# Scan layers of a hybrid network: every engine issues in the program's order instead of the scheduler's order

## Chip, cores, metric

The kernel runs on one core of a Trainium2 chip. The metric is the device time of the execution in microseconds (us). A program on one core has no second core to compare itself with, so the state of a run is read from its time and its granted TensorE clock; every run told here was a fast one and gave the reference's result.

Engines are named as in the profile: PE is TensorE's matmul, PEld its weight load, DVE is VectorE, ACT is ScalarE, POOL is GpSimd and SP is SyncE.

## The reference

Two layers with a selective scan over images of 64 x 64, then two attention and feed-forward layers on the same pixels as tokens. Only the scan layers are touched. Per image (four of them), per layer:

```python
xs = [x_hw, x_wh, x_hw reversed, x_wh reversed]          # k: four directions, L = 4096
dts, B, C = split(einsum("kdl,kcd->kcl", xs, x_proj))     # 6, 16, 16
delta = softplus(einsum("krl,kdr->kdl", dts, dt_w) + dt_b)
h = exp(delta * A) * h + delta * B * u                    # one step along L, 192 x 16 states
y = (h * C).sum(states)                                   # summed over the directions
```

and then a normalisation, a gate silu(z) and an output projection.

## The kernel before

An image is 32 **scan steps**: four directions k, each of eight chunks of 512 pixels. A step has six **groups** g0 to g5 (halves h of the channels, blocks i of the states). A group passes through all engines. The program writes the stages of different groups in a software pipeline: while group n is scanned, n-1 is weighed by C, n-2 is summed, n-3 is kept, and the next step's inputs are made in three small pieces per group. The scheduler may reorder the instructions of an engine where no data forbids it, and did so.

```python
p_da = ...bufs=4, space=PSUM     # exp(delta*A), one bank per tile of a group
p_y = ...bufs=1, space=PSUM      # y_ps
p_b = ...bufs=2, space=PSUM      # b_ps
p_one = ...bufs=1, space=PSUM    # "ps1": everything else on PE
...
def chunk_inputs(xc, k, c, got):           # a generator: each yield is one piece
    u = scan_view(xc, k, c)                # strided in the transposed directions
    got["b"] = p_b.tile(...); c_ps = p_one.tile(...)
    ... four matmuls with bc_w: b, then c
    yield
    got["c"] = cp.tile([128, TC], F32, name="cc", bufs=2)
    nc.scalar.copy(got["c"], c_ps)
    yield
    for m in range(2):
        raw = p_one.tile([128, TC], F32, name="ps1")
        ... two matmuls with dl_w (L229)
        yield
        nc.scalar.activation(top[:, m], raw, AF.Relu, ...)
        nc.scalar.activation(e[:, m], raw, AF.Abs, ...)
        yield
    ... ACT: exp, ln, identity             # yield
    nc.vector.scalar_tensor_tensor(w, ...) # L244; yield
    nc.gpsimd.tensor_tensor(...)           # x2, delta; yield; yield
    ... du = delta * u on DVE (L253), and its transfer to DRAM

class Group:
    def scan(self):
        for t in range(NT):                # NT = 4
            da = p_da.tile([128, TC], F32, name="da")
            nc.tensor.matmul(da, cst.rep[part, i], self.got["delta"][part, h], ...)
        for t, da in enumerate(das):
            nc.scalar.activation(da, da, AF.Exp, scale=a_col[...])
        for t in range(NT):
            nc.vector.tensor_tensor(st[:, t], st[:, t], self.got["b"], ALU.mult)
        for t, da in enumerate(das):
            nc.vector.tensor_tensor_scan(st[:, t], da, st[:, t], 0.0 if c == 0 else col, ...)
    def weigh(self):
        if c < NC - 1:
            nc.scalar.copy(self.carry[...], st[:, :, TC - 1])
        for t in range(NT):
            nc.gpsimd.tensor_tensor(st[:, t], st[:, t], self.got["c"], ALU.mult)
    def sum(self):
        if i == 0:
            y_of[h] = p_y.tile([P, TC], F32, name="y_ps")
        ... four matmuls into y_of[h]
    def keep(self):                        # only after the third block, i == 2
        nc.vector.tensor_tensor(to, to, rows(y_of[h]), ALU.add)
...
def stages(n):
    for back, stage in ((1, "weigh"), (3, "keep"), (2, "sum")):
        getattr(flat[n - back], stage)()
for n in range(len(steps)):
    ahead = chunk_inputs(xc, *steps[n + 1], inputs[n + 1])
    for at in range(n * 6, (n + 1) * 6):
        ... load the states of later groups
        flat[at].scan()
        stages(at)
        for _ in range(3):
            next(ahead, None)
```

Of the kernel before, what the change touches and what calls it, by code (L numbers as in the profile page):

```python
# [57 lines left out]
def rows(t):  # L58

    if len(t.shape) == 2:  # L60
        return t.rearrange("p (r w) -> p r w", w=HW)
    return t.rearrange("p h (r w) -> p h r w", w=HW)


class Consts:
# [29 lines left out]
def ssm_layer(ctx: ExitStack, tc, cst, a, pre, x_in, x_out):  # L95

    nc = tc.nc
# [45 lines left out]
    for k in range(K):  # L143
        for h in range(2):
# [7 lines left out]
            )  # L152
            nc.scalar.copy(dl_w[:, k, h], ps[:, : 2 * P])

    stats_of = {}

    def conv(b):
# [7 lines left out]
        for c in range(NC):  # L165
            mid = xn[:, 1 + ROWS * c : 1 + ROWS * (c + 1), 1 : 1 + HW]
            nc.sync.dma_start(mid, rows(x_in[b, :, c * TC : (c + 1) * TC]))
            nc.vector.bn_stats(st[:, c, :], mid)  # L168
# [20 lines left out]
        for c in range(NC):  # L189
            for h in range(2):  # L190
                ps = p_one.tile([128, TC], F32, name="ps1")
                for tap in range(9):
                    dy, dx = divmod(tap, 3)
                    nc.tensor.matmul(  # L194
                        rows(ps),
                        taps[:, tap, h * P : (h + 1) * P],
                        xn[:, ROWS * c + dy : ROWS * (c + 1) + dy, dx : dx + HW],
                        start=tap == 0,
                        stop=tap == 8,
                    )  # L200
                nc.scalar.activation(  # L201
                    xc[:, h, c * TC : (c + 1) * TC], ps, AF.Silu, bias=conv_b[:, h : h + 1]
                )
        return xc

    def chunk_inputs(xc, k, c, got):
# [5 lines left out]
        for m, ps in enumerate((got["b"], c_ps)):  # L212
            for h in range(2):
                nc.tensor.matmul(rows(ps), bc_w[:, k, h, m], u[:, h], start=h == 0, stop=h == 1)  # L214
# [45 lines left out]
    class Group:  # L260
# [6 lines left out]
        def __init__(self, k, c, h, i, got, carry, xc, y):  # L267
            self.k, self.c, self.h, self.i = k, c, h, i
            self.got, self.carry, self.xc, self.y = got, carry, xc, y
# [293 lines left out]
def body(tc, a, out):  # L563
    nc = tc.nc
    with ExitStack() as ctx:
        cst = Consts(nc, ctx.enter_context(tc.tile_pool(name="const", bufs=1)), a)
        dram = ctx.enter_context(tc.tile_pool(name="dram", bufs=1, space=DRAM))
        x1 = dram.tile([B, C, L], F32, name="x1")
        x2 = dram.tile([B, C, L], F32, name="x2")
        ssm_layer(tc, cst, a, "L0_", a["x"], x1)  # L570
        ssm_layer(tc, cst, a, "L1_", x1, x2)
        token_layers(tc, cst, a, ["L2_", "L3_"], x2, out)
# [85 lines left out]
```

## Time and profile before

| | before |
|---|---|
| time, median of 2 | 17766.17 us (17765.54 to 17766.8) |
| busy: PE, DVE, ACT, POOL | 14593.3, 13631.7, 7698.0, 8983.9 us |
| one scan step, median of the eight images | 51.84 us |
| from an image's last scan to the next one's first, median | 358.2 us |
| mean PE clock | 0.716 |

A "step" is the time from the first scan of an image to the end of its last, over 32. PE has the highest busy share, but DVE is what the scan waits for. The busy times in the four directions of the first image show it. The columns of this view are the stretch, its length in us, the busy us (and instructions) of PE, PEld, DVE, ACT and POOL, then the PE clock, the busy share of the DMA engines and GB/s. Before:

```profile
214.74:614.51 399.77, 353.74 (x866) 96.09 (x870) 382.49 (x421) 185.78 (x306) 274.08 (x206) 0.69 0.60 133
614.51:1042.61 428.10, 378.34 (x904) 94.37 (x900) 397.56 (x425) 192.07 (x315) 280.79 (x208) 0.72 0.57 126
1042.61:1454.00 411.39, 367.38 (x908) 100.56 (x900) 388.79 (x428) 192.49 (x314) 278.68 (x208) 0.68 0.59 131
1454.00:1873.20 419.20, 368.18 (x866) 89.61 (x862) 387.71 (x416) 200.58 (x318) 274.43 (x205) 0.72 0.55 121
```

Length less DVE's busy time, over eight steps, is DVE's stall per step: 2.2, 3.8, 2.8 and 3.9 us. Directions 2 and 4 read the image transposed.

### The profile page before, as it was taken

Reading aid. Unit: us, or ns where it says so; the run is one execution under the profiler, and the core shown is the slowest. Engines: PE = TensorE matmul, PEld = TensorE weight load, DVE = VectorE, ACT = ScalarE, POOL = GpSimd, SP = SyncE. Lnnn points to the kernel's source line nnn. Section 1 sums busy time; section 2 is a strip of 40 time slices with the busy share of each in tenths; the row PEclk is TensorE's granted clock in tenths of the full one; section 3 lists DMA queues with packets and bytes.
Section 4 is the critical chain, followed back from the end, with each engine's and each line's share of the span. In section 5 each row is a group of like instructions: output and inputs, shape, how many; then the busy total and the mean of one; then the engine's idle time right before and its main releaser. Section 6 shows DMA issues by size and latency. Waiting matters only on the chain.

```text
span 17763.9 us, 120237 instructions
## 1 busy us (share of the span) xinstructions
PE 14593.3 (82%) x34144; PEld 4171.9 (23%) x34144; DVE 13631.7 (77%) x15421; ACT 7698.0 (43%) x12017; POOL 8983.9 (51%) x6700
## 2 busy tenths in 40 slices
PE   8888788887888788887888788887888788885555
PEld 2222222222222222222222222222222222222222
DVE  5999399975999489984999579993999669993333
ACT  3444344443444344442444344442444334444555
POOL 3666166653666266652666356661666346660000
PEclk8767777667767777677776777677767777676665
DMA  4555165543555155542555255552555345550000
GB/s 88 129 128 128 40 133 129 128 98 74 129 128 129 41 126 129 128 106 62 133 124 131 60 109 127 130 122 48 131 128 129 71 96 128 129 126 23 7 7 7
DMA packets 360991, 1786.21 MB, mean 101 GB/s; under 512 B 93550, under 2 KB 94960, under 8 KB 162760
## 3 DMA queue, kind: packets, MB, share of 16 engines
q1 hardware_dynamic: 353160, 1765.94, 44.8%
q10 hardware_dynamic: 7168, 12.59, 0.2%
q8 instruction: 275, 4.51, 0.1%
q14 instruction: 388, 3.18, 0.1%
HBM read 1658.82 MB, written 119.54 MB: 100 GB/s over the span
## 4 chain that ended last, share of the span: by engine, by line
PE 41%; POOL 18%; DVE 17%; issue 15%; ACT 9%; DMA 0%; DVEq 0%; POOLq 0%; SPq 0%; ACTq 0%
POOL st L306 13%; PE da L285 11%; DVE st L297 9%; PE y_ps L313 8%; PE ps L194 6%; PE b_ps L214 5%; PE ps L229 4%; DVE st L293 3%; POOL delta L248 3%; POOL t L246 3%; ACT L88 1%; ACT da L291 1%; PE ps L362 1%; PE ps L370 1%; PE y_ps L383 1%
## 5 line engine op out<-in xcount | busy, mean ns | idle before, releaser
L306 POOL TENSOR_TENSOR st<-st,cc 128x512 f32<-128x512 f32 x6144 | 7785.6, 1298 | 4253.5 <-ACT carry L304 2489.1
L297 DVE TENSOR_TENSOR_SCAN st<-da,carry,st 128x512 f32<-128x512 f32 x5376 | 6460.2, 1264 | 662.8 <-ACT da L291 661.6
L285 PE MATMUL da<-delta,rep 32*128 32x512 f32 x12288 | 5498.9, 884 | 812.6 <-DVE st L297 723.7
L291 ACT ACTIVATE da<-da,A_logs 128x512 f32<-128x512 f32 x6144 | 3907.5, 664 | 4885.7 <-PE da L285 4876.1
L313 PE MATMUL y_ps<-st,sel 128*32 128x512 f32 x12288 | 3321.2, 913 | 798.5 <-POOL st L306 626.8
L293 DVE TENSOR_TENSOR st<-st,b_ps 128x512 f32<-128x512 f32 x6144 | 3788.2, 678 | 0.0
L285 PEld LDWEIGHTS da<-delta,rep 32*128 32x128 f32 x12288 | 1744.2, 245 | 4783.9 <-DVE st L297 3466.9
L229 PE MATMUL ps<-xc,dl_w 128*128 128x512 f32 x2048 | 1445.5, 834 | 23.5 <-ACT cc L217 12.6
L313 PEld LDWEIGHTS y_ps<-st,sel 128*32 128x32 f32 x12288 | 486.1, 137 | 3388.2 <-POOL st L306 1708.4
L246 POOL TENSOR_TENSOR t<-t,t 128x1024 f32<-128x1024 f32 x256 | 603.3, 2357 | 1047.5 <-DVE t L244 1047.5
L194 PE MATMUL ps<-xn,taps 96*128 96x512 f32 x2304 | 1047.4, 609 | 93.2 <-ACT xc L201 68.4
L214 PE MATMUL b_ps<-xc,bc_w 128*128 128x512 f32 x1024 | 980.8, 1052 | 73.5 <-DVE st L293 73.5
L253 DVE TENSOR_TENSOR du<-delta,xc 128x512 f32<-128x512 f32 x512 | 870.3, 1739 | 178.3 <-POOL delta L248 177.7
L237 ACT ACTIVATE t<-ps,dt_projs_bias 128x512 f32<-128x512 f32 x512 | 351.7, 687 | 1373.1 <-PE ps L229 1324.1
L297 DVE TENSOR_TENSOR_SCAN st<-da,st 128x512 f32<-128x512 f32 x768 | 876.2, 1201 | 50.5 <-ACT da L291 49.9
L214 PE MATMUL ps<-xc,bc_w 128*128 128x512 f32 x1024 | 874.4, 987 | 27.9 <-ACT t L238 21.7
L160 POOL MEMSET xn<- 96x66 f32 x8 | 1.2, 150 | 1762.7 <-PE ps L194 1598.0
L168 DVE BATCH_NORM_STATS2 st<-xn 96x6 f32<-96x512 f32 x64 | 44.2, 690 | 871.9 <-DMA xn<-x 437.2
L244 DVE SCALAR_TENSOR_TENSOR t<-t,t 128x1024 f32<-128x1024 f32 x256 | 329.3, 1286 | 426.0 <-ACT t L242 426.0
L484 POOL MEMSET tn<- 1x4096 f32 x8 | 28.0, 3506 | 1194.7 <-PE pa L525 1027.6
L229 PEld LDWEIGHTS ps<-xc,dl_w 128*128 128x128 f32 x2048 | 398.0, 205 | 949.8 <-issue 600.4
L248 POOL TENSOR_TENSOR delta<-t,t 128x1024 f32<-128x1024 f32 x256 | 600.7, 2347 | 3.1
(118 smaller groups left out, 8712.8 us busy)
## 6 DMA issues: line engine op xcount, KB each, us to landing
st<-scratch SPq DMA_DIRECT2D x1536, 1024.0 KB
scratch<-du SPq DMA_DIRECT2D x1024, 96.0 KB
xr<-in_x SPq DMA_DIRECT2D x64, 192.0 KB
x<-xr ACTq DMA_DIRECT2D x64, 192.0 KB
xr<-x SPq DMA_DIRECT2D x64, 192.0 KB
xn<-in_x SPq DMA_DIRECT2D x32, 192.0 KB
xn<-x SPq DMA_DIRECT2D x32, 192.0 KB
t<-x SPq DMA_DIRECT2D x4, 1536.0 KB
```

The costliest lines, as they stand in the source:

```text
L194: nc.tensor.matmul(rows(ps), taps[:, tap, h * P : (h + 1) * P], xn[:, ROWS * c + dy : ROWS * (c + 1) + dy, dx : dx + HW], start=tap == 0, ...
L214: nc.tensor.matmul(rows(ps), bc_w[:, k, h, m], u[:, h], start=h == 0, stop=h == 1)
L229: nc.tensor.matmul(rows(raw), dl_w[:, k, h, m * P : (m + 1) * P], u[:, h], start=h == 0, stop=h == 1,)
L246: nc.gpsimd.tensor_tensor(ln, ln, w, ALU.subtract)
L248: nc.gpsimd.tensor_tensor(delta, top, ln, ALU.add)
L253: nc.vector.tensor_tensor(rows(du[:, h]), rows(delta[:, h]), u[:, h], ALU.mult)
L285: nc.tensor.matmul(da, cst.rep[part, i], self.got["delta"][part, h], start=True, stop=True)
L291: nc.scalar.activation(da, da, AF.Exp, scale=a_col[:, k, h, j : j + 1])
L293: nc.vector.tensor_tensor(st[:, t], st[:, t], self.got["b"], ALU.mult)
L297: nc.vector.tensor_tensor_scan(st[:, t], da, st[:, t], 0.0 if c == 0 else col, ALU.mult, ALU.add)
L306: nc.gpsimd.tensor_tensor(st[:, t], st[:, t], self.got["c"], ALU.mult)
L313: nc.tensor.matmul(y_of[h][32 * t : 32 * t + 32], cst.sel[:, i], self.st[:, t], start=i == 0, stop=i == NB - 1,)
```

## The change

The intent is to let the program, which is written as a pipeline with small pieces, say in which order each engine issues. After the setup of a layer, `nc` becomes a wrapper. Each call through it adds an ordering edge from the engine's previous wrapped instruction to this one; the edge stays within one engine. No arithmetic, tile or transfer changes: the traces count the same instructions on PE, DVE and POOL, and 1786 MB moved in both. What the compiler adds by itself does change. ACT has 935 table loads in place of 1031, and there are 16903 semaphore instructions in place of 14921.

```diff
+class InOrder:
+    def __init__(self, tc, engine):
+        self.tc, self.engine = tc, engine
+
+    def __getattr__(self, name):
+        call = getattr(self.engine, name)
+
+        def ordered(*args, **kwargs):
+            ins = call(*args, **kwargs)
+            self.tc.keep_in_program_order(ins)
+            return ins
+
+        return ordered
+
+
+class Engines:
+    def __init__(self, tc):
+        for name in ("tensor", "vector", "scalar", "gpsimd", "sync"):
+            setattr(self, name, InOrder(tc, getattr(tc.nc, name)))
@@ ssm_layer, after the setup of the weights
+    nc = Engines(tc)
     stats_of = {}
```

In all profiles of the changed kernel the wrapped instructions carry the line of the helper, L75. They are told apart by tile.

## The prediction

> **What bounds the kernel now.** I read, in order: the page's slices, the waits of VectorE (DVE), and the timeline of one scan step. The slices give the stages:
>
> ```profile
> DVE  5999399975999489984999579993999669993333
> POOL 3666166653666266652666356661666346660000
> PEclk8767777667767777677776777677767777676665
> ```
>
> One digit is 444 us. The pattern repeats every 2017 us, eight times (two layers, four images): about 1660 us of scan with DVE at 9 tenths, then some 356 us of finish, convolution and first inputs in which DVE is mostly idle. The last 1553 us are the token layers, which the change does not touch. TensorE's (PE's) clock is about 0.7, neither full nor half.
>
> A scan step (32 an image, 256 in all) has six groups g0 to g5. In each, DVE does 4 multiplies (spaced 2.39 us together in the timeline) and 4 scans (4.72), 7.11 us; a step adds two "keep" adds, one L244 and two L253. In the windows of the four directions DVE is busy 48.2 to 49.0 us of each step, and a step lasts 51.3 to 53.3. So DVE bounds the scan, with about 3 us of stall a step. The waits say where (total us, times, longest):
>
> ```profile
> DVE st L297 <- ACT da L291: 711.5, 425, 3.8
> DVE du L253 <- POOL delta L248: 177.7, 192, 4.9
> ```
>
> 711.5/256 = 2.8 us a step: DVE waits for an exponential of ScalarE (ACT). The timeline of a step in the second direction (start, us, engine, line) shows one such wait whole:
>
> ```profile
> 659.89 3.42 PE L285 MATMUL da<-delta,rep 32*128 32x512 f32 x6
> 662.23 1.22 DVE L337 TENSOR_TENSOR y<-y,y_ps 128x512 f32<-128x512 f32 x1
> 662.59 0.19 ACT L304 COPY carry<-st 128x4 f32<-128x4 f32 x1
> 662.85 4.96 POOL L306 TENSOR_TENSOR st<-st,cc 128x512 f32<-128x512 f32 x4 [1.67 <-ACT carry L304]
> 663.55 1.93 PE L313 MATMUL y_ps<-st,sel 128*32 128x512 f32 x8 [0.24 <-issue]
> ...
> 667.84 0.58 ACT L217 COPY cc<-ps 128x512 f32<-128x512 f32 x1 [3.82 <-POOL st L306]
> ...
> 671.18 3.61 PE L229 MATMUL ps<-xc,dl_w 128*128 128x512 f32 x4
> ...
> 674.72 1.14 PE L285 MATMUL da<-delta,rep 32*128 32x512 f32 x8
> ...
> 676.67 4.81 DVE L297 TENSOR_TENSOR_SCAN st<-da,carry,st 128x512 f32<-128x512 f32 x4 [3.75 <-ACT da L291]
> ```
>
> ACT's copy of cc waits until GpSimd (POOL) has weighed the step's last group, the delta matmuls L229 wait for that copy (one PSUM buffer, "ps1"), the next da matmuls stand behind them, and DVE's scan waits 3.75 us. Note what the scheduler did first: three of the four da matmuls of g0 (659.89, x6, two instructions each) and the carry copy ran ahead of y_ps at 663.55, which had to wait for DVE's keep (662.23 to 663.45).
>
> **What the Trainium skill says.** "PSUM — Partial Sum Buffer", Engine vs sequencer instructions: ScalarE, VectorE and GpSimdE queues are strict FIFO, and matmuls start and complete in program order. So an instruction that waits holds up everything behind it on its engine; the 3.05 to 3.82 us of ACT before cc agree. "TensorE: Matmul & The Clock Gate", Part 1: the PE clock has a half state and a full state, half after some 3.4 us of idleness. The trace agrees on the states: in one-us windows the clock is 0.50 or 1.00, eight y_ps instructions take 1.94 us or 1.06, four da 2.09 or 1.14. It agrees less on time: from 706 to 723 the clock stays at 0.50 though PE is recorded as mostly busy. Matmuls on xc in the transposed directions take 3.7 us for four in either state; otherwise 1.98 at full and up to 3.6 at half.
>
> **The change part by part.** It adds and removes no arithmetic, tile or transfer. It pins each engine's order to that in which the program calls. I compared both orders engine by engine. Transfers are the same in the scan. DVE's order hardly differs. PE and ACT lose every hoist: PE always does four da of group n, then four y_ps of n-2, then the next step's inputs; ACT does four exponentials, then the carry of n-1, then its input work. I follow one step by hand with the durations above, PE at half speed first.
>
> *g5 to g0.* The single y_ps bank makes y_ps wait for keep, which is behind g5's scans on DVE. All four da of g0 now stand behind it. From the end of keep: y_ps 1.94, da 2.09, first exponential 0.66, hand-overs 0.1: 4.8 us. DVE has 2.39 us of multiplies. Stall 2.4 (full clock 0.6; now nearly 0).
>
> *g0 to g1.* From that first exponential: three more 1.7, only then the carry 0.2, POOL's four products 4.95, cc with its hand-over 0.7: 7.6. In the transposed directions the b and c matmuls (7.4 in all) end later still, so 8.9. Then L229 with its load 3.9 (transposed) or about 3.0, da 1.14 to 2.09, exponential 0.76. Sum 14.7 transposed, 13.0 otherwise. DVE has 4.72 + 2.39 = 7.1. Stall 7.6 or 5.9 (before: 3.75 and 1.12 in the steps shown by the timeline). The reason is that the carry copy, which releases POOL, comes seven us later than now.
>
> *g1 to g2.* Relu and abs of the first L229 half now come after four exponentials and the carry: 1.7 + 0.2 + 1.27 = 3.2. Then the second half 3.9 or 3.0, da 1.14 or 1.6, exponential 0.76: 9.0 or 8.6, against 7.1. Stall 1.9 or 1.5. Now none, as ACT takes relu and abs first.
>
> *g2 to g3.* L244 waits about 0.6 for ACT's chain (1.06, table load 1.28, 1.15, 1.13), and keep, y_ps, da again make 0.5. *g3 to g5.* The single da matmuls follow the scans of the group before; POOL is ready; the transfers keep their 15 us of lead. No stall.
>
> Sum: 13.0 transposed, 10.9 otherwise, mean 12 us of stall a step against about 3.4 now (the two waits quoted): +8.6, times 256 = **+2200 us**. With PE at full speed throughout, the same sums give 9.5 and 5.7, mean 7.6: +4.2, or +1080 us. PE idles about seven us before keep releases it, so the first chain should run at half speed; the truth should lie nearer the first.
>
> *Between images.* (a) Six of the sixteen z matmuls now run inside the scan; pinned, all follow it: 6 x 2.76 = +16. (b) In the normalisation chunks mu of chunk c+1 ran under chunk c; now it follows the output matmul: about 2.6 x 8 = +21. (c) The next image's eight statistics were made long before; now they stand behind the last chunk on DVE: 8 x 0.64 plus the small chain that had been done early, less waits, +9. (d) The first multiply need not wait behind the second step's inputs: -4. Sum +42, times 8 = **+340 us**.
>
> 17766 + 2200 + 340 = 20300; at full clock 17766 + 1080 + 340 = 19190. I predict **20150 us**, +13%.
>
> **Rivals.** *The scheduler's order is the bad one, and program order removes its stalls.* The program interleaves input work in small pieces as if to be issued as written. For it: the trace has 3.4 us of stall a step, and DVE's floor of 49 us would give 256 x 3 = 770 us less, about 17000 with all stalls gone. Against it: the largest stall now has the same cause in program order (cc behind POOL, L229 behind cc), and the carry comes later, not sooner. *Off the path: DVE bounds, its order hardly changes, so nothing happens.* It needs da to stay ahead of DVE as now, with four PSUM buffers as slack; then only the ends of the images count, 17766 + 340 = 18100, or 2% slower. Against: the slack is 2.4 us of multiplies where y_ps waits for keep, and the waiting chain is 4.8. *A transfer becomes the bound*, if in-order SyncE holds a load behind another: its order in the scan is unchanged and a longer step gives it more time, so it would make no difference.
>
> **Range and chances.** The low end, 19000, is PE at full clock and the image ends somewhat better hidden than I count; the high end, 20900, is half clock in every chain plus about 600 us of waits that I missed. Faster by 2% needs the stalls to go, against the order I read: 0.03. Within 2% needs the second rival: 0.04. Slower: 0.93.
>
> **What would show each step right or wrong.** Right: in the waits, DVE's scan on the exponentials grows from 711 to some 2800 us; DVE's busy time stays near 13630 and its slices fall from 9 to 8; in a step's timeline the stalls stand before the scans of g0, g1 and g2, that of g1 longest; POOL's wait on carry and PE's y_ps wait on DVE's keep grow; a step takes 59 to 63 us. Image ends grow by about 42 us. Wrong: a step under 55 us; g0's scan without a wait (then y_ps does not block da); a carry copy soon after the scan before it; or the token stage longer than 1553 us, which I take as unchanged.

## The result, and the profile after

The changed kernel takes 19968.44 us (median of 2, 19963.87 to 19973.01), against 17766.17. The ratio is 1.124, with a 95% interval of 1.1191 to 1.1288: **slower by 12.4%**, inside the predicted range. Ratios here are the mean time of one kernel's fast runs over that of the other's of the same rounds, so not quite the ratio of the medians quoted.

| | before | after |
|---|---|---|
| one scan step, median of the eight images | 51.84 us | 59.7 us |
| from an image's last scan to the next one's first, median | 358.2 us | 384.6 us |
| from the last image's last scan to the end | 1742.5 us | 1759.3 us |
| DVE busy, whole execution | 13631.7 us | 13710.8 us |
| mean PE clock | 0.716 | 0.697 |

The sum of it: the scans of the eight images grew by 2012 us together (251 each); the seven gaps grew by 175 us together (six within the layers by 26.3 each, that between the layers by 17.5), the last end by 17, and the first scan began 5 us sooner. That is about 2200 us, of which 92% is in the scan.

The slices of the changed kernel, DVE's row and the PE clock:

```profile
DVE  5888388874888568883888658883788748885333
PEclk7666766667666776667666676667666676666666
```

Where the scan had nines for DVE it has eights. The same view of the four directions as shown for before:

```profile
209.34:674.49 465.15, 318.76 (x876) 81.43 (x876) 384.90 (x424) 190.99 (x311) 281.89 (x208) 0.67 0.53 118
674.49:1171.06 496.57, 335.53 (x896) 78.80 (x896) 402.09 (x425) 193.06 (x315) 286.62 (x208) 0.70 0.49 109
1171.06:1636.15 465.09, 315.88 (x904) 79.33 (x896) 385.08 (x425) 192.91 (x315) 282.04 (x208) 0.68 0.52 115
1636.15:2121.08 484.93, 333.22 (x864) 78.87 (x856) 394.73 (x417) 185.49 (x304) 279.43 (x205) 0.68 0.47 104
```

DVE has almost the same work. Its stall is now 10.0, 11.8, 10.0 and 11.3 us a step, 10.8 in the mean against 3.2 before. The waits (us in total, times, longest) say what it stalls for:

```profile
POOL st L75 <- ACT carry L75: 5655.7, 896, 22.1
DVE st L75 <- ACT da L75: 2588.7, 829, 8.3
```

Before, the second of these (L297 on L291, shown in the prediction) was 711.5 us, and the first was:

```profile
POOL st L306 <- ACT carry L304: 2489.1, 759, 9.6
```

So DVE's wait for the exponentials rose from 711.5 to 2588.7 us, and POOL's for the carry copy from 2489.1 to 5655.7. A stretch of a step in the second direction (start, us, engine; in brackets the idle time just before and what ended it; weight loads and what the chain does not need are left out):

```profile
1045.36 1.22 DVE L75 TENSOR_TENSOR y<-y,y_ps 128x512 f32<-128x512 f32 x1
1046.68 1.93 PE L75 MATMUL y_ps<-st,sel 128*32 128x512 f32 x8 [6.21 <-POOL st L75]
1048.54 2.09 PE L75 MATMUL da<-delta,rep 32*128 32x512 f32 x8
1050.65 2.39 ACT L75 ACTIVATE da<-da,A_logs 128x512 f32<-128x512 f32 x4 [9.37 <-PE da L75]
1051.34 4.81 DVE L75 TENSOR_TENSOR_SCAN st<-da,carry,st 128x512 f32<-128x512 f32 x4 [2.39 <-ACT da L75]
...
1052.94 0.21 ACT L75 COPY carry<-st 128x4 f32<-128x4 f32 x1
1053.23 4.97 POOL L75 TENSOR_TENSOR st<-st,cc 128x512 f32<-128x512 f32 x4 [6.95 <-ACT carry L75]
1055.82 3.61 PE L75 MATMUL ps<-xc,bc_w 128*128 128x512 f32 x4
1059.52 0.58 ACT L75 COPY cc<-ps 128x512 f32<-128x512 f32 x1 [6.37 <-PE ps L75]
1060.16 3.68 PE L75 MATMUL ps<-xc,dl_w 128*128 128x512 f32 x4 [0.73 <-ACT cc L75]
1063.77 2.09 PE L75 MATMUL da<-delta,rep 32*128 32x512 f32 x8
...
1066.57 4.81 DVE L75 TENSOR_TENSOR_SCAN st<-da,carry,st 128x512 f32<-128x512 f32 x4 [8.05 <-ACT da L75]
```

Read it downward as one chain. PE idles 6.21 us at the head of its queue. The profile puts that down to POOL, but y_ps starts right as DVE's keep ends (1045.36 + 1.22 = 1046.58), because keep empties the only y_ps bank. All four da of g0 stand behind y_ps, the first exponential behind them, and DVE's scan waits 2.39 us. Then c, cc, L229 and g1's da follow each other on PE and ACT one by one, and g1's scan waits 8.05 us. Before, three of g0's da and the carry copy had gone ahead.

### The profile page after: what moved, and what is told of

Same layout as the page of the kernel before. It is cut to its first block, busy times and chain, and to the rows that moved or that the text cites. A ratio compares the mean times of both kernels' runs of the same rounds, so it can differ in the third digit from the quotient of the medians.

```text
span 19962.1 us, 122123 instructions
## 1 busy us (share of the span) xinstructions
PE 13310.0 (67%) x34144; PEld 3653.7 (18%) x34144; DVE 13710.8 (69%) x15421; ACT 7601.1 (38%) x11921; POOL 9121.2 (46%) x6700
## 5 line engine op out<-in xcount | busy, mean ns | idle before, releaser
L75 POOL TENSOR_TENSOR st<-st,cc 128x512 f32<-128x512 f32 x6144 | 7894.6, 1318 | 5841.7 <-ACT carry L75 5655.7
L75 DVE TENSOR_TENSOR_SCAN st<-da,carry,st 128x512 f32<-128x512 f32 x5376 | 6454.6, 1261 | 2349.4 <-ACT da L75 2347.7
L75 ACT ACTIVATE da<-da,A_logs 128x512 f32<-128x512 f32 x6144 | 3812.6, 663 | 7072.6 <-PE da L75 7072.4
L75 PE MATMUL da<-delta,rep 32*128 32x512 f32 x12288 | 4805.3, 993 | 769.9 <-DVE st L75 633.7
L75 PE MATMUL y_ps<-st,sel 128*32 128x512 f32 x12288 | 2852.5, 911 | 3145.5 <-POOL st L75 1953.2
L75 DVE TENSOR_TENSOR st<-st,b_ps 128x512 f32<-128x512 f32 x6144 | 3777.0, 673 | 85.1 <-DMA st<-scratch 85.1
L75 PE MATMUL ps<-xc,dl_w 128*128 128x512 f32 x2048 | 1703.2, 969 | 1115.2 <-ACT t L75 679.1
L75 PEld LDWEIGHTS da<-delta,rep 32*128 32x128 f32 x12288 | 1382.7, 275 | 4310.3 <-DVE st L75 3037.4
L75 POOL TENSOR_TENSOR t<-t,t 128x1024 f32<-128x1024 f32 x256 | 604.5, 2361 | 3058.3 <-DVE t L75 2783.9
L75 DVE SCALAR_TENSOR_TENSOR t<-t,t 128x1024 f32<-128x1024 f32 (+1 forms) x320 | 446.7, 1396 | 1408.5 <-ACT t L75 1406.3
L75 PEld LDWEIGHTS y_ps<-st,sel 128*32 128x32 f32 x12288 | 360.9, 133 | 5541.6 <-POOL st L75 2917.9
L75 PE MATMUL ps<-xn,taps 96*128 96x512 f32 x2304 | 1044.7, 608 | 118.6 <-ACT xc L75 93.3
L75 DVE TENSOR_TENSOR_SCAN st<-da,st 128x512 f32<-128x512 f32 x768 | 875.3, 1199 | 241.1 <-ACT da L75 241.1
L75 ACT ACTIVATE t<-ps,dt_projs_bias 128x512 f32<-128x512 f32 x1024 | 653.8, 697 | 904.5 <-PE ps L75 904.5
L75 ACT ACT_TABLE_LOAD x678 | 869.9, 1283 | 84.0 <-DVE xr L75 46.9
L75 PEld LDWEIGHTS ps<-xc,dl_w 128*128 128x128 f32 x2048 | 461.1, 249 | 2185.0 <-ACT t L75 920.9
L75 DVE TENSOR_TENSOR du<-delta,xc 128x512 f32<-128x512 f32 x512 | 822.3, 1646 | 39.0 <-POOL delta L75 39.0
L75 PE MATMUL b_ps<-xc,bc_w 128*128 128x512 f32 x1024 | 739.9, 851 | 0.0
L75 PE MATMUL ps<-xc,bc_w 128*128 128x512 f32 x1024 | 702.9, 814 | 0.0
L75 ACT COPY cc<-ps 128x512 f32<-128x512 f32 x256 | 149.8, 585 | 1358.5 <-PE ps L75 833.1
L75 ACT ACTIVATE t<-t 128x1024 f32<-128x1024 f32 (+1 forms) x448 | 426.9, 953 | 619.7 <-DVE t L75 616.9
L75 POOL TENSOR_TENSOR delta<-t,t 128x1024 f32<-128x1024 f32 x256 | 600.0, 2344 | 20.1
```

What stands on the lines that cost most here:

```text
L75: ins = call(*args, **kwargs)
```

## The experiments

Before the first of them there were two theories. **The order**, theory Q in the texts: the loss is instructions that stand behind a blocked one on their own queue, on PE and ACT, in three places (g0 behind keep; g1 behind carry, cc and L229; g2 behind relu and abs). The rival, **theory P** in some of the texts: pinning costs something by itself, through the edges or because nothing can be hoisted (issued earlier than written) any more, whatever the order. If the order is it, moving single calls in the program's text, with all pins kept, must take single stalls away; if the pins are it, it must not. All times are of several rounds against the kernel before on the same chip, whose medians were 17762 to 17765 us. The edits are shown cut to their core. The last two columns are medians over the images.

| run | median us | ratio to before (95%) | us per step | us between images |
|---|---|---|---|---|
| keep_first | 19222 | 1.0822 (1.0806 to 1.0838) | 56.9 | 380.7 |
| carry_first | 19451 | 1.0952 (1.0936 to 1.0969) | 57.6 | 385 |
| relu_early | 19545 | 1.1004 (1.0988 to 1.1020) | 58.1 | 382.8 |
| cc_three_buffers | 19639 | 1.1057 (1.1039 to 1.1075) | 57.85 | 401.6 |
| inputs_spread | 18752 | 1.0557 (1.0542 to 1.0573) | 55.07 | 381 |
| spread_b_early | 17919 | 1.0087 (1.0072 to 1.0102) | 51.9 | 378 |
| all_pinned | 16904 | 0.9517 (0.9503 to 0.9531) | 48.04 | 374.4 |
| all_free | 18066 | 1.0172 (1.0155 to 1.0189) | 53.35 | 347.6 |
| all_scan_pinned | 16718 | 0.9413 (0.9399 to 0.9427) | 48.03 | 350.7 |
| rest_pinned | 17380 | 0.9784 (0.9769 to 0.9799) | 49.8 | 378.1 |
| pe_pinned | 18577 | 1.0457 (1.0440 to 1.0474) | 54.5 | 374.5 |
| scan_pins_only | 19671 | 1.1072 (1.1055 to 1.1088) | 59.7 | 343.5 |

### keep_first: the keep add ahead of the group's multiplies

```diff
+                if at >= 3:
+                    flat[at - 3].keep()
                 flat[at].scan()
                 stages(at)        # without keep
```

> The changed kernel with one program line moved: the keep add of group n-3 is called before group n's multiplies and scans, all pins kept. Theory Q (the loss comes from instructions that wait at the head of a pinned queue): the y_ps matmuls no longer wait for DVE, the stall before g0's scan (2.39 us in the trace) and the 0.3 us before g3's go, the one before g1's scan stays near 7 us; 57 us a step, 256 x 2.7 = 690 us less: 19280. Theory P (pins cost by themselves, through added waits and instructions, whatever the order): no change, 19970. Theory N (the step is bound elsewhere and the wait only moves to g1): within 0.5% of 19970.

It took 19222 us, 746 less than the changed kernel. The timeline of its DVE in the second direction:

```profile
1000.36 1.22 DVE L75 TENSOR_TENSOR y<-y,y_ps 128x512 f32<-128x512 f32 x1
...
1003.87 4.80 DVE L75 TENSOR_TENSOR_SCAN st<-da,carry,st 128x512 f32<-128x512 f32 x4
...
1026.00 4.81 DVE L75 TENSOR_TENSOR_SCAN st<-da,carry,st 128x512 f32<-128x512 f32 x4 [7.87 <-ACT da L75]
```

A scan in the place of the 2.39 us wait has none, as y_ps and da are done sooner; the long wait before g1 is as it was (7.87). One instruction of DVE, moved by one group's work, released PE. So g0's stall is keep's, and it is one of several. Over all steps DVE has no idle time left before g0's scan, where it had 2.2 us in the mean. One expected gain failed to come: the stall before g3 did not go, it rose from 0.9 to 1.5 us.

### carry_first: the carry copy of group n-1 ahead of the exponentials of n

```diff
                 das.append(da)
+            if before is not None:
+                before.save_carry()     # the copy, taken out of weigh()
             for t, da in enumerate(das):
```

> The changed kernel with the carry copy of group n-1 called ahead of the exponentials of group n, all pins kept. Theory Q, as the prediction told it (a late carry is why POOL, then cc, then the delta matmuls are late): the stall before g1's scan falls by about 2.5 us in the untransposed directions, where POOL gates cc; in the transposed ones the c matmuls (b and c take 7.4 us) gate cc nearly as late, so there it falls by under 1 us. Mean 1.2 to 1.6 us a step, 300 to 400 us: 19570 to 19670. If the late carry were the whole cause of that stall, some 4 us a step: 18950. Theory P: 19970.

It took 19451 us, 517 less, more than expected. In the second direction g1's stall did not change in the steps read; in the third it went from 6.74 to 1.48. Over all steps its mean fell from 6.8 to 6.6 us in the transposed directions and from 5.4 to 2.3 in the others. The cc copy and g1's scan in the second direction:

```profile
1030.15 0.59 ACT L75 COPY cc<-ps 128x512 f32<-128x512 f32 x1 [6.70 <-PE ps L75]
...
1037.20 4.81 DVE L75 TENSOR_TENSOR_SCAN st<-da,carry,st 128x512 f32<-128x512 f32 x4 [8.27 <-ACT da L75]
```

and g1's scan in the third, in the changed kernel and in this run:

```profile
3531.17 4.81 DVE L75 TENSOR_TENSOR_SCAN st<-da,carry,st 128x512 f32<-128x512 f32 x4 [6.74 <-ACT da L75]
```

```profile
3428.27 4.81 DVE L75 TENSOR_TENSOR_SCAN st<-da,carry,st 128x512 f32<-128x512 f32 x4 [1.48 <-ACT da L75]
```

So the wait for POOL through the carry copy sets g1 where the image is read straight. Where it is read transposed, the b and c matmuls (3.6 to 3.8 us for four instructions each) end later than POOL, and cc waits for PE instead. Two chains run side by side there, and shortening one does nothing.

### relu_early: relu and abs of the first delta half already in g0

```diff
-                for _ in range(3):
+                for _ in range((4, 2, 3, 3, 3, 3)[at % 6]):
                     next(ahead, None)
```

> The changed kernel with the input work cut 4, 2, 3 pieces for g0, g1, g2 in place of 3, 3, 3: relu and abs of the first delta half are called in g0, ahead of g1's exponentials. Theory Q: the stall before g2's scan (2.26 us) falls to under 0.8, the others stay; 1.5 us a step, 380 us: 19590. Theory P: 19970.

It took 19545 us, 424 less. g2's scan in the second direction, in the changed kernel:

```profile
1011.74 4.81 DVE L75 TENSOR_TENSOR_SCAN st<-da,carry,st 128x512 f32<-128x512 f32 x4 [2.26 <-ACT da L75]
```

and the scans of g1 and g2 in this run:

```profile
1040.97 4.81 DVE L75 TENSOR_TENSOR_SCAN st<-da,carry,st 128x512 f32<-128x512 f32 x4 [8.09 <-ACT da L75]
...
1048.07 4.80 DVE L75 TENSOR_TENSOR_SCAN st<-da,carry,st 128x512 f32<-128x512 f32 x4
```

g2's stall of 2.26 us is gone and g1's stays. The three edits, each alone, sum to 746 + 517 + 424 = 1687 of the 2200 us.

### cc_three_buffers: cc need not wait for POOL

```diff
-        got["c"] = cp.tile([128, TC], F32, name="cc", bufs=2)
+        got["c"] = cp.tile([128, TC], F32, name="cc", bufs=3)
...                                   # to make room: xr bufs=2 becomes bufs=1
```

> The changed kernel with three buffers for cc in place of two, so that its copy needs no product of POOL to be done; one buffer for xr in place of two to make room, which costs only the finish of each image (at most some 15 us each, 120 in all). Theory Q: ACT's wait of cc on POOL (525 us) goes to nil; the stall before g1's scan falls as for carry_first, only where POOL gates cc: 1.2 us a step, 300 us, less the finish: 19670 to 19790. If POOL's product were what holds that stall in all directions: 18950. Theory P: 19970 or more.

It took 19639 us, 330 less. The wait that it aims at, in the changed kernel and in this run:

```profile
ACT cc L75 <- POOL st L75: 525.3, 104, 5.1
```

```profile
ACT cc L75 <- POOL st L75: 51.9, 20, 2.9
```

The steps gain 1.8 us each, 467 us over 256; the gaps between images are 17 us longer each, put down to the single xr buffer. The same link that carry_first shortens is here cut, with a like result in the scan: g1's mean stall falls from 5.4 to 2.2 us where the image is read straight, and from 6.8 to 6.6 where transposed.

### inputs_spread: the input pieces reordered

The pieces of the next step's inputs come one per group: g0 first delta half with its relu and abs, g1 the second, g2 exp, ln, identity, L244 and POOL's two, g3 du and its transfer, g4 c and cc, g5 b.

```diff
-        ... b, c matmuls; yield; cc copy; yield     # at the head
         ... delta halves, exp/ln, delta, du         # fewer yields
+        ... c matmuls; cc copy; yield; b matmuls    # at the end
-                for _ in range(3):
-                    next(ahead, None)
+                next(ahead, None)
```

> The changed kernel with the next step's input work called in another order, one matmul block a group: first delta half and its relu and abs in g0, second half in g1, the softplus chain in g2, du and its transfer in g3, c and cc in g4, b in g5; all pins kept, keep and carry where they were. Theory Q: the stalls before g1's and g2's scans (about 7 and 2 us) go, the 2.4 us before g0's and about 1 us before g3 stay; 52.4 us a step against 59.7: 18100. Theory P (pins cost by themselves): 19970. Theory B (PE's total work in the transposed directions is the bound): the stall only moves to g2 to g5, 19500.

It took 18752 us, not the expected 18100. A wait that neither kernel had came up, and the timeline of one step shows how:

```profile
DVE st L75 <- PE b_ps L75: 1356.1, 248, 5.8
```

```profile
1025.99 1.21 DVE L75 TENSOR_TENSOR y<-y,y_ps 128x512 f32<-128x512 f32 x1
1027.31 1.93 PE L75 MATMUL y_ps<-st,sel 128*32 128x512 f32 x8 [7.15 <-issue]
1029.17 3.79 PE L75 MATMUL b_ps<-xc,bc_w 128*128 128x512 f32 x4
...
1032.99 2.48 DVE L75 TENSOR_TENSOR st<-st,b_ps 128x512 f32<-128x512 f32 x4 [5.79 <-PE b_ps L75]
```

The b matmuls in g5 are written behind y_ps, which is blocked until keep; so DVE's first multiply of the step waits 5.79 us for b. I had moved one head-of-line blocking away and written another.

### spread_b_early: the same with the b matmuls in g3

```diff
+        ... b matmuls       # ahead of du in g3
         ... du and its transfer; yield
         ... c matmuls; cc copy
-        yield; b matmuls
```

> inputs_spread (18752, where 18100 was expected) with b called in g3 in place of g5. In inputs_spread DVE's multiplies wait 1356 us in all, 5.3 us a step, for b_ps, which is pinned behind the y_ps matmuls that wait for keep. Theory Q: that wait goes, the scan of g0 waits 2.4 us for its exponentials again; 256 x 2.9 = 740 us less: 18010. Rival (PE has no room for b in g3 either, or the step is bound by the transposed matmuls): 18750.

It took 17919 us, 833 less than inputs_spread and close to what was expected. The wait for b is gone. What is left on the exponentials is 826.0 us over 496 times, the longest 2.4, which is keep's. That settles the miss above.

### all_pinned: keep_first, carry_first and inputs_spread together, all pins

> keep first, carry first and spread inputs together, all pins kept. Theory Q: no queue head waits on the path any more; DVE's own 49 us a step plus under 1 us: 49.8; 18 scans' worth of images as in the changed kernel (gaps of 384 us): 19970 - 256 x 9.9 = 17430, 2% under the kernel before. Theory P: above the kernel before, 17766, as the image gaps alone are 26 us longer each.

It took 16904 us, 15% less than the changed kernel and 4.8% less than the one before: better than expected. Keep ahead of the multiplies also frees y_ps for b, so the wait of inputs_spread vanishes here too. Of the scan's waits on the exponentials 9.5 us are left in the whole execution. A part of the gain was not foreseen: DVE's own work fell from 48.7 us a step in the kernel before to 48.0, as du (1809 to 1524 ns in the mean) and L244 (1291 to 1203) run shorter here.

### all_free: the same text without the pins

```diff
-    nc = Engines(tc)
```

> The same calls as all_pinned without any pin: the scheduler orders. Theory Q: the order decides and not the pins; if the scheduler keeps near the call order the step is 50 to 51 us and the image gaps are those of the kernel before: 17250 to 17500. If it hoists again as in the kernel before, 51.8 a step: 17700. Theory P: clearly faster than all_pinned.

It took 18066 us, 1.7% above the kernel before, with 1481.3 us of DVE's wait for exponentials back. With the text of all_pinned, pins make it 1162 us faster. So theory P falls: in the scan the pins cost nothing that shows, and with a good order they are worth 6.4%, because the scheduler does not keep the written order and finds a worse one (5.9 us of stall a step against less than 0.1). Nor do the pins by themselves bring the semaphore instructions that the changed kernel has more: all_pinned has 15890, all_free 16058.

### all_scan_pinned: pins in the scan alone

```diff
-    nc = Engines(tc)
+    free, nc = tc.nc, Engines(tc)
-    def conv(b):
+    def conv(b, nc=free):
-    def finish(b, xc, y):
+    def finish(b, xc, y, nc=free):
```

> all_pinned with the pins in the scan steps alone, conv and finish left to the scheduler. Theory Q: steps as in all_pinned (49.8 us), image gaps near those of the kernel before (358 us) in place of 384: 17430 - 8 x 24 = 17240, 3% under the kernel before. If the scheduler needs the scan unpinned to place finish work inside it: no better than all_pinned.

It took **16718 us, 5.9% less than the kernel before**, the fastest of all runs. DVE's slices, and the busy times in the scan of one image:

```profile
DVE  5999399975999399974999489984999489983333
```

```profile
2089.00:3626.00 1537.00, 1438.21 (x3560) 381.41 (x3560) 1535.74 (x1689) 766.56 (x1253) 1132.96 (x829) 0.76 0.63 138
```

DVE is busy 1535.74 of 1537 us: the scan is at the floor that this DVE work sets. What is won over all_pinned lies between the images, 350.7 us in place of 374.4 (and 1736 in place of 1762 after the last), where the scheduler may mix the end of one image with the start of the next.

### scan_pins_only: the changed kernel, with image ends left to the scheduler

The same edit of `conv` and `finish`, but on the changed kernel's own order.

> The changed kernel with conv and finish unpinned. Theory Q: steps stay at 59.7 us; the gaps between images fall from 384 to some 355 us, eight times 26 to 29: 19740 to 19760. If the pinned image ends were what hurts: near 17800.

It took 19671 us. The step stays at 59.7 us, the gap falls to 343. So the pins of the image ends cost about 300 us, and the scan's order makes the rest. The gap is now below the 358.2 us of the kernel before.

### rest_pinned and pe_pinned: pins on some engines

```diff
-            setattr(self, name, InOrder(tc, getattr(tc.nc, name)))
+            e = getattr(tc.nc, name)
+            setattr(self, name, InOrder(tc, e) if name in ('vector', 'gpsimd', 'sync') else e)
```

> The changed kernel's calls with DVE, POOL and SyncE pinned, PE and ACT left to the scheduler. Theory Q: the loss is all in PE's and ACT's order; steps within 1 us of the kernel before's 51.8, gaps partly longer (the statistics stay pinned on DVE): 17770 to 17950. Theory P (pins cost by themselves): three of five engines pinned, at least half of the loss: 18900.

With DVE, POOL and SP pinned and PE and ACT free it took 17380 us: 2.2% *faster* than the kernel before, where I had expected about the same. The wait on the exponentials:

```profile
DVE st L75 <- ACT da L316: 450.0, 296, 3.8
```

It is 450.0 us against 711.5. So none of the loss comes from the order of DVE, POOL or SP by itself; it needs PE's or ACT's. The trace shows where the 2.2% lie: of 2.0 us gained a step, 1.4 are stall (the one before g4 falls from 1.4 to 0.2 us in the mean) and 0.6 DVE's own work. Which of the three pins does it was not isolated.

pe_pinned has `('tensor',)` in that list.

> PE alone pinned. Theory Q: PE's order makes the stall before g0's scan (2.4 us) and, in the transposed directions, most of the one before g1's (b, c and the first delta half ahead of da); with ACT free the carry and relu may go first again, as in carry_first and relu_early (517 and 424 us): about 19968 - 900 = 19050. If ACT's order made most of the loss: under 18500.

It took 18577 us, 4.6% over the kernel before. PE's order by itself makes part of the loss, not all. The mean stalls show which part: 1.9 us before g0, and 4.8 before g1 in the transposed directions (2.4 in the kernel before); before g1 in the others (1.1) and before g2 (none) there is no more than in the kernel before. This is not a clean share: with PE pinned, the scheduler put the free engines in another order than before, in 120 places 11 multiplies of DVE in a row. ACT alone was never pinned, so how the loss divides between PE and ACT stays open, and since the chains run through both, a division may not mean much.

## Why the prediction was right

**The direction and its cause** hold. PE and ACT lost their hoists, the stalls came where they were expected, and theory P and the rival of "off the path" fell.

**g5 to g0**: 2.4 us predicted, 2.39 and 2.38 measured, at half clock as assumed (y_ps 1.93, da 2.09). keep_first takes it away alone.

**g0 to g1**: 7.6 transposed and 5.9 otherwise predicted; 8.05 and 6.78 in neighbouring steps of the second direction, 6.74 in the third. The split into two chains, b and c in one case and POOL in the other, is what carry_first shows.

**g1 to g2**: 1.9 and 1.5 predicted, 2.26 and 1.11 measured; relu_early takes it away alone. **g2 to g3**: 1.1 predicted (0.6 for L244 and 0.5 more), 0.32 and 0.33 in one step of the second direction, 0.92 before L244 and none after in the third. **No stall in g4 and g5** held, as did "no transfer becomes the bound". The mean over all steps of the trace (DVE's idle time up to the group's last scan, in us) beside the prediction:

| stall | g0 | g1 | g2 | g3 | sum |
|---|---|---|---|---|---|
| transposed, predicted | 2.4 | 7.6 | 1.9 | 1.1 | 13.0 |
| transposed, measured | 2.3 | 6.8 | 1.7 | 0.9 | 11.7 |
| otherwise, predicted | 2.4 | 5.9 | 1.5 | 1.1 | 10.9 |
| otherwise, measured | 2.2 | 5.4 | 1.3 | 0.9 | 9.8 |

**The sum** was one microsecond too large: 12 us of stall a step against 10.8 measured, 3.4 before against 3.2. So +8.6 became +7.6 of stall, plus 0.3 of DVE's own time, which makes the measured +7.9 and 2012 us in place of 2200. The 0.3 is L244's: 1583 ns in the mean against 1291, as 224 of 248 now run beside POOL where 24 of 240 did; du got shorter (1677 against 1809). The stalls of the steps read by hand sum to 12.1 to 13.4 in the second direction, while its mean is 11.8: one or two steps were taken for all, and steps differ. All four terms were a little too large, g1's the most. One reading of the start was loose too: in the windows shown above DVE is busy 47.8 to 49.7 us a step and a step lasts 50.0 to 53.5, not 48.2 to 49.0 and 51.3 to 53.3; the stall of about 3 us is the same.

**The image ends** are the term that was mis-sized: 42 us for each predicted, 26 measured where an image follows in the same layer, 340 in all against about 190 (the seven gaps and the last end). The traces tell which part, by the same marks in the first gap of both kernels, in us from the last scan's end:

| mark | before | after | added since the mark above | predicted |
|---|---|---|---|---|
| first matmul of the means | 30.0 | 51.7 | 21.6 | (a) 16 |
| last output added | 169.2 | 194.9 | 4.1 | (b) 21 |
| first convolution matmul | 171.8 | 205.1 | 7.6 | (c) 9 |
| last convolution matmul ends | 314.5 | 347.6 | -0.2 | |
| next scan | 358.2 | 384.8 | -6.5 | (d) -4 |

So (c) and (d) came about as counted, (a) a little dearer (all 16 z matmuls now run after the scan), and (b), the mean of the next chunk behind the output matmul, is the part that was too large: 4 us, about 0.5 a chunk, where 21 were counted at 2.6 a chunk. The token layers did not get longer (1573 us from the last output to the end before, 1566 after).

Both terms erred upward, and 20150 was already set a little below the sum of 20300; the truth lay 182 us lower still. The rival "program order removes its stalls" was wrong for this program, but its floor was near: 17000 us with all stalls gone was named, and 16904 was reached by changing the program's order, with the pins kept. That the two lie so close is partly luck: DVE's own work fell by some 175 us, which was not in the count, and the pinned image ends cost some 115, which was not either.

## What to carry to other kernels

Pinning the issue order is neither good nor bad: it makes the written order real, and every call that may wait then holds back all calls written behind it on its engine. Before pinning, go down each engine's written order and ask for each instruction whose turn it blocks: a consumer that frees a single buffer (keep) belongs first, a short copy that releases another engine (carry) belongs ahead of long work, and what the next group needs must not be written behind what waits for a later event. With such an order, pinned in the scan alone, this kernel is 5.9% faster than the one before; the same text as all_pinned left to the scheduler is 1.7% slower. Where a stage has no written pipeline, as at the image ends here, the scheduler did better.

## What the Trainium skill lacked or had wrong

- "PSUM — Partial Sum Buffer", Engine vs sequencer instructions, states the FIFO order of the queues and the matmuls, and no run here contradicts it. It does not say what it costs when the head of the queue waits for a single PSUM buffer: here 2.39 us a step before g0's scan, and 746 us of the execution by keep_first.
- "TensorE: Matmul & The Clock Gate", Part 1: the two clock states agree (0.50 and 1.00). All stretches at one clock but one in each trace last a whole multiple of 3.413 us. The page's time to the full clock, one busy window of about 3.4 us, is not confirmed: in the kernel before, from 708 to 722 us, the clock stood at 0.50 while PE was recorded busy for 13.7 of the 14 us. The ends of matmuls are modelled, though, and two blocks of eight da there are spread over 5.59 and 4.79 us where eight take 2.09 elsewhere at the same clock, so PE may have been less busy than recorded. Many of these matmuls also use 32 rows or columns of the array. No run tested either reason.
- "SBUF — State Buffer" names a penalty for accesses that step to a new line of 16 bytes, but no page that I found has its cost for a matmul's moving operand: four matmuls on xc took 3.68 us in the transposed direction at a clock of 1.00, and 1.98 us untransposed.
- "SBUF — State Buffer", Who interferes with whom, describes the port that DVE and GpSimd share for DVE instructions with two SBUF inputs. The trace of the kernel before agrees: beside POOL's work a du takes 1.74 us in the median where the image is read straight and 2.09 where transposed, without it 0.68 and 1.03 (8 and 16 cases), so 1.06 us more in both. The page gives no number by which to count this ahead.
- "ScalarE: Activation LUTs", What ACT_TABLE_LOAD costs: the load of about 1283 ns agrees (1.28 us). The drain of about 1380 ns added there is not seen: in the changed kernel an activation ends at 1014.51, a load starts at 1014.53 and the next activation at 1015.82.
